# Order of the first transfers and place of one weight's columns in a four-layer graph network kernel

## The chip, the cores and the metric

The kernel runs on one core of a Trainium2 chip. The metric is device time in microseconds (us) of that core, as the median of several executions. One further execution was taken by the hardware profiler; every row and duration below that is called a row of the profile comes from it.

The engines are named as the profile names them: PE is the matrix engine (TensorE), with PEld for its weight loads; DVE is VectorE; ACT is ScalarE; POOL is GpSimd; SP is SyncE, which here only issues transfers (DMAs). Each engine works through its own list of instructions in order and waits at an instruction until its semaphores are there. A DMA is issued by SP, ACT or POOL, each with its own queue; the transfers of all queues run on the same 16 DMA engines.

## The reference, cut to what matters

32 graphs of 512 nodes with 256 features pass through four layers. Each layer normalizes, applies a relu, and adds the result of its graph attention to x. Only layers 0 and 1 bear on the change:

```python
# layer 0: 4 heads of 64
h = jnp.maximum(_layernorm(x, axis=-1), 0.0)
Wh = (X @ W).reshape(B, N, H, F)
e_src = jnp.einsum('bnhf,hf->bnh', Wh, a_src)
e_dst = jnp.einsum('bjhf,hf->bjh', Wh, a_dst)
e = jax.nn.leaky_relu(e_src[:, :, None, :] + e_dst[:, None, :, :], LRELU_ALPHA)
e = jnp.where(mask, e, NEG_INF)
alpha = jax.nn.softmax(e, axis=2)
Hout = jax.nn.elu(jnp.einsum('bijh,bjhf->bihf', alpha, Wh))
# layer 1: one head of 256, softmax over the other axis
h = jnp.einsum('bnf,fo->bno', x, W)
s1 = h @ a1
s2 = h @ a2
e = jax.nn.leaky_relu(s1[:, :, None] + s2[:, None, :], negative_slope=ALPHA)
```

Since `(h W) a = h (W a)`, the scores s1 and s2 can be had as two more columns of the weight: W a1 and W a2. The kernel works these columns out once, at its start, for layer 0 (8 columns) and for layer 1 (2 columns). Layer 2 is another attention over products of h, and layer 3 a transformer block with its own, larger weights.

## The kernel before, in words

All work of the 32 graphs is written out as jobs of a plan (class `Plan`). A job belongs to one engine and has a place, a number; `plan.graph(b)` takes the places of graph b from a table (`PLACES`, with tables of their own for the first three and the last three graphs in `OWN`), and `plan.aside(place)` gives one fixed place to the jobs that follow. `carry_out` sorts all jobs by place and issues them in that order, with a tie from each job to the one before it on the same engine, so that each engine's order within the plan is the table's. What is issued outside the plan (the first loads on ACT's queue, the columns of the weights at L683 to L697) is put among it by the program builder by its own priorities.

Neighbouring graphs overlap: while one graph is in its PE-heavy layer 3, the next ones are in layers 0 to 2.

The start of the program, which the change touches:

- ACT's queue gets six loads in this order: w0 (`w0_t`), w1 (`w1_t`), the rows `src_r` and `dst_r` of layer 0, the rows `a1_r` of layer 1, and the small `a2_t`. A "row" load reads one row of memory once for each of the 128 partitions (`rows_of`, L35). w0 and w1 are 256 KB, `src_r` and `dst_r` 128 KB, `a1_r` 256 KB.
- SP's queue gets graph 0's adjacency (1024 KB), then x of graph 0 (512 KB), then x of graphs 1 and 2, then the transposes of graph 0's mask. The table gives the first two of them place 0, and adjacency comes first since it is the first job of the two.
- POOL's queue gets the weights of layer 3 and other constants (the list `late`, 3.94 MB), each held until x of graph 0 has landed (`plan.load(..., lambda: first)`, where `first` is the job that loads x of graph 0).
- DVE works out the columns: for each half k of the rows of w0, a product with `src_r` or `dst_r` into the scratch tile `wa` (L688) and a sum over each head (L689); for w1, a product with one half of `a1_r` (L694) and a sum (L697). Scratch `wa` is one tile, so a sum always comes between two products.
- DVE also takes the statistics of x for the first norm (`norm_stats`): four `bn_stats` (BATCH_NORM_STATS2 in the profile), four `bn_aggr`, then, after two steps of ACT on `rstd`, three small steps on `newton` and `rstd` and one on `shift`. ACT then writes h of graph 0 in four parts.
- ACT makes the mask `m` from the adjacency as soon as that has landed; SP turns it into `mT` with four transposing DMAs.
- PE transposes h (`ps_t`), multiplies by w0 with its columns (`ps_wh`), and turns the source scores into rows (`ps_sp`, copied by DVE to `spr`, written to memory as `rows_d`, and read back as `rows`, once for each partition). DVE then makes the weights p out of rows, the other scores and mT, and PE multiplies them (`ps_oT`, `ps_den`).
- A few products on PE (`ps_warm`, list `WARM`) are there only to keep PE busy.

Each helper records its operations under one line: L215 for all of ACT's, DVE's and most of POOL's jobs in the plan, L236 for SP's DMAs, L244 for the late weights, L266 for transposes and L268 for products on PE.

Of the kernel before, what the change touches and what calls it, by code (L numbers as in the profile page):

```python
# [11 lines left out]
F32 = mybir.dt.float32  # L12
# [4 lines left out]
OP = mybir.AluOpType  # L17
AX = mybir.AxisListType

P = 128  # L20
# [14 lines left out]
def rows_of(nc, pool, ap, n, name, tag=None, bufs=None, load=None):  # L35

    t = pool.tile([P, n], F32, tag=tag or name, name=name, bufs=bufs)
    (load or nc.scalar.dma_start)(t, bass.AP(tensor=ap.tensor, offset=ap.offset, ap=[[0, P], [1, n]]))
    return t
# [9 lines left out]
def weight_of(nc, pool, ap, name, extra=0, load=None):  # L49

    k, m = ap.shape
    t = pool.tile([P, k // P, m + extra], F32, name=name)
    (load or nc.scalar.dma_start)(t[:, :, :m], ap.rearrange("(k p) m -> p k m", p=P))
    return t
# [229 lines left out]
def width(args):  # L284
# [48 lines left out]

OWN = {
    0: [
        0, 0, 0, 106563, 309, 1073, 1073, 3182, 47382, 297632, 53499, 245689, 52704, 0, 0, 0, 0, 0, 0, 0, 0, 0, 0,
        0, 0, 0, 0, 0, 0, 0, 0, 0, 0, 0, 0, 0, 0, 0, 0, 0, 7, 7, 7, 7, 7, 7, 7, 7395, 1121, 0, 232, 258, 232, 232,
        232, 2502, 1493, 635, 635, 730, 635, 5936, 765, 8516, 3266, 1050, 1050, 1050, 2440, 2440, 17625, 13746,
        2440, 1632, 1889, 1889, 4537, 7572, 7833, 7388, 7395, 7880, 7395, 8585, 9886, 11802, 13679, 12762, 13540,
        13752, 13707, 15308, 14272, 13966, 13966, 16994, 13966, 16169, 16249, 16583, 18584, 18163, 18872, 19087,  # L340
        18927, 18927, 20349, 20349, 20349, 20349, 20352, 20409, 20838, 20907, 20907, 21387, 21387, 21387, 22329,
        23457, 20725, 20923, 23457, 25982, 33376, 34261, 34261, 37292, 34867, 36474, 39879, 41011, 39696, 39709,
        46106, 46400, 46400, 46400, 46675, 46675, 46675, 46675, 49427, 59065, 55989, 56768, 56768, 65040, 68466,
        47867, 47867, 67836, 67836, 69041, 77635, 79329, 79329, 68466, 72704, 72704, 72280, 91934, 91934, 92968,
        92968, 92968, 104578, 95599, 145914, 104578, 105186, 108990, 114563, 157733, 166027, 173427, 174141, 136956,
        151172, 165888, 173979, 136722, 147431, 150754, 153574, 136357, 147891, 158851, 171074, 190479, 191171,
        191171, 196527, 196605, 183067, 183067, 186603, 186603, 187082, 206651, 196694, 196694, 187082, 193870,
        201947, 201947, 187262, 197716, 201947, 206129, 206129, 206129, 207622, 208026, 208026, 208352, 208026,
        219854, 210838, 220497, 220913, 220913, 227229, 217998, 217998, 217998, 226715, 229449, 227967, 229449,
        233286, 233286, 247339, 247339, 247339, 250551, 250856, 251751, 251803, 249399, 228019, 237297, 252726,  # L350
        252726, 252726, 256033, 256033, 256033, 268130, 246835, 246835, 261876, 261876, 261876, 271725, 297107,
        261876, 240354, 240790, 253683, 253683, 253683, 255019, 301246, 309901, 318155, 274295, 278428, 294941,
        305600, 318055, 318055, 299511, 305359, 305359, 320090, 318173, 320554, 305359, 321266, 318173, 321267,
        320641, 321267, 321267, 321267, 321267, 321863, 321863, 326043, 329227, 331562, 332202, 332561, 332561,
        332561, 332922, 330548, 330759, 332506, 332661, 335150, 332802, 406651, 341220, 341466, 342050, 344077,
        344077, 344077, 338280, 338280, 341180, 350371, 353293, 359563, 344829, 344829, 345290, 352882, 355803,
        351180, 351355, 351355, 351355, 360418, 344308, 344308, 344391, 347079, 344345, 350100, 362932, 344061,
        344061, 344061, 344061, 344061, 348875, 362932, 353485, 342050, 343799, 343799, 343799, 343799, 348486,
        365222, 358873, 348973, 348973, 348973, 360911, 348973, 367027, 369940, 367027, 367027, 367638, 367879,
        367879, 385037, 382465, 382465, 394363, 397797, 363107, 363107, 363107, 364066, 363107, 367844, 388551,  # L360
        364560, 364560, 365934, 364560, 370478, 377727, 389387, 379253, 362319, 362411, 362354, 362538, 363348,
        367831, 392522, 386227, 370565, 370565, 370565, 386534, 371732, 387162, 392760, 387162, 393047, 393047,
        396335, 396414, 392760, 398262, 398545, 398803, 406052, 462858, 397797, 406052, 406052, 406052, 407196,
        398293, 406183, 406183, 406183, 407281, 407235, 407281, 407281, 407281, 407235, 407313, 407522, 407522,
        407522, 407522, 407522, 407522, 407522, 407522, 412250, 408973, 413187, 413155, 412853, 413187, 413187,
        413187, 412853, 413349, 413590, 413590, 414897, 416013, 436150, 436742, 421541, 421541, 423055, 415478,
        418099, 421341, 426237, 426237, 427146, 418315, 419286, 419286, 415750, 417007, 417007, 415424, 416349,
        419708, 424205, 424205, 424205, 421266, 421266, 422615, 430070, 430330, 430330, 432660, 432660, 432660,
        432660, 432927, 433724, 433724, 436311, 439075, 439075, 439075, 439075, 439075, 441195, 430355, 430355,
        439081, 440598, 440598, 440653, 440653, 440653, 440653, 440653, 440653, 440653, 440890, 440890, 440972,  # L370
        440977, 443515, 442768, 441195, 443964, 443964, 443964, 441195, 443964, 443964, 443964, 443972, 444016,
        444016, 444016, 444016, 444148, 444142, 444730, 444016, 455955, 462911, 463054, 441529, 533896, 458476,
    ],
    1: [
        -83597, -100000, -83597, 170797, -79776, -79776, -60271, -57701, -52873, 201135, -52847, 76061, 156221,
# [222 lines left out]
def quick_path(  # L598
# [5 lines left out]
    nc = tc.nc  # L604
    B, N, D = x.shape
    NT = N // P
    KD = D // P
# [10 lines left out]
    const = ctx.enter_context(tc.tile_pool(name="const", bufs=1))  # L618
    act = ctx.enter_context(tc.tile_pool(name="act", bufs=1))
# [15 lines left out]
    plan = Plan(tc, PLACES, OWN)  # L635

    def new(tag, name, shape, dtype=F32):
        return plan.tile(K[tag], name, shape, dtype)
# [15 lines left out]
    nc.gpsimd.memset(nshift, -SHIFT)  # L654

    w0_t = weight_of(nc, const, w0, "w0_t", 2 * H0)
    w1_t = weight_of(nc, const, w1, "w1_t", 2)
    src_r = rows_of(nc, act, a0_src, D, "src_r", "half_0")
    dst_r = rows_of(nc, act, a0_dst, D, "dst_r", "half_1")
    a1_r = rows_of(nc, act, a1, 2 * D, "a1_r", "half_2")  # L660
    a2_t = const.tile([P, KD], F32, name="a2_t")
    nc.scalar.dma_start(a2_t, a2[0].rearrange("(k p) o -> p (k o)", p=P))

    late = []

# [19 lines left out]
    for k in range(KD):  # L685
        for a_r, at, sign in ((src_r, D, -1.0), (dst_r, D + H0, 1.0)):
            wa = act.tile([P, N], F32, tag="half_3", name="wa", bufs=1)
            nc.vector.scalar_tensor_tensor(wa[:, :D], w0_t[:, k, :D], sign, a_r, OP.mult, OP.mult)  # L688
            nc.vector.tensor_reduce(  # L689
                w0_t[:, k, at : at + H0], wa[:, :D].rearrange("p (h f) -> p h f", h=H0), AX.X, OP.add  # L690
            )
        for at, sign in ((0, 1.0), (1, -1.0)):
            wa = act.tile([P, N], F32, tag="half_3", name="wa", bufs=1)
            nc.vector.scalar_tensor_tensor(  # L694
                wa[:, :D], w1_t[:, k, :D], sign, a1_r[:, at * D : (at + 1) * D], OP.mult, OP.mult
            )
            nc.vector.tensor_reduce(w1_t[:, k, D + at : D + at + 1], wa[:, :D], AX.X, OP.add)  # L697


    FULL, HALF = 0.858, 0.4315  # L700
# [394 lines left out]
        all_within(seen, graph_mv[0])  # L1095


    plan.aside(max(OWN[0][:2]) + 1)
    for tile_, source in late:
        plan.load(tile_, source, lambda: first)  # L1100
    for place, products in WARM:
# [5 lines left out]
    for b in range(B):  # L1107
        plan.graph(b)
        adj_t = new("adj", f"adj_{b}", [P, NT, N], I32)
        plan.dma(adj_t, adj[b].rearrange("(t p) j -> p t j", p=P), 3.4)  # L1110
        x_t = new("x", f"x_{b}", [P, NT, D])
        job = plan.dma(x_t, x[b].rearrange("(t p) d -> p t d", p=P), 2.0)
        if b == 0:
            first = job
        seen = new("seen", "seen", [P, UPPER])
        graph_mv = [new("mv", "mv", [P, 6, NT, 2]), 0]
        mT, m3 = masks(b, adj_t, seen)
        layer0(b, x_t, mT, seen)
        x_t = layer1(b, x_t, mT, seen)
        layer2(b, x_t, mT, seen)  # L1120
        if b == 0:
            ready = plan.at
        layer3(b, x_t, m3, seen)
# [506 lines left out]
```

## Time and profile before

| What | Value |
|---|---|
| median of 3 runs | 3402.93 us (3396.50 to 3409.46) |
| the profiled execution's own time | 3401.32 us |
| its span, from the first to the last instruction | 3399.4 us |
| PE, DVE, ACT, POOL busy | 3337.5, 2823.3, 2115.3, 11.1 us |
| first instruction of PE | 22.40 us |
| h of graph 0 starts on ACT | 21.69 us |
| graph 0's row copy `spr` | 31.52 us |
| first `ps_oT` of graph 0 | 41.33 us |

Times in rows are counted from the span's start. A row of the timeline gives the start, the length, the engine, the line, the operation, what it writes and reads, how many there are, and in brackets how long its engine stood idle before it and what ended that. "PEclk" in a table of stretches is the granted clock of TensorE, "DMA share" the mean busy share of the 16 DMA engines. In a view of the DMA queues, q1 is SP's, q10 ACT's and q0 POOL's. A row of the chain of waits gives start, length and work of the chain that ended last, followed back from the last instruction to what released it.

The profile as a whole shows PE busy in nine tenths or more of each fortieth of the span but the first and the last:

```profile
## 2 busy tenths in 40 slices
PE   6999999999999999999999999999999999999998
PEld 4565666555665655655655656556556556565555
DVE  6887888888888888888888888888888888887785
```

### The profile page before, as it was taken

To read this page: it belongs to the slowest core of one execution; us is meant where nothing else is said; L and a number is where in the kernel's file an instruction comes from. 1 tells how busy PE (TensorE), PEld (TensorE's weight loads), DVE (VectorE), ACT (ScalarE), POOL (GpSimd) and SP (SyncE) were. 2 spreads that over 40 slices of the span, in tenths; PEclk is the share of its full clock that TensorE was granted. 3 is DMA by queue.
4 is the path that set the end of the run, shared out by engine and by line. 5 is a ranking of instruction groups with operands and counts; after the bars stand their busy time and mean duration, and the time that the engine had idled before them with its cause. 6 is when DMAs were issued, how large, how long until landed. Compare 5 with 4: busy or idle time off the path is not lost.

```text
span 3399.4 us, 48314 instructions
## 1 busy us (share of the span) xinstructions
PE 3337.5 (98%) x17842; PEld 1973.6 (58%) x17842; DVE 2823.3 (83%) x5499; ACT 2115.3 (62%) x4801; POOL 11.1 (0%) x25
## 2 busy tenths in 40 slices
PE   6999999999999999999999999999999999999998
PEld 4565666555665655655655656556556556565555
DVE  6887888888888888888888888888888888887785
ACT  5756666556676556676566665566765667655563
POOL 1000000000000000000000000000000000000000
PEclk9999999999999999999999999999999999999999
DMA  5112110112111111111111112111112111110000
GB/s 165 43 46 57 51 51 28 54 46 57 51 35 40 57 47 57 51 33 42 53 51 51 41 34 57 46 57 51 35 40 65 51 51 42 28 52 26 20 8 27
DMA packets 161171, 161.16 MB, mean 47 GB/s; under 512 B 92576, under 2 KB 126880, under 8 KB 156832
## 3 DMA queue, kind: packets, MB, share of 16 engines
q1 hardware_dynamic: 158464, 153.00, 15.5%
q0 software_dynamic: 1216, 3.94, 0.4%
q8 instruction: 143, 2.34, 0.3%
q10 hardware_dynamic: 1248, 1.05, 0.1%
q14 instruction: 100, 0.82, 0.1%
HBM read 122.96 MB, written 18.22 MB: 42 GB/s over the span
## 4 chain that ended last, share of the span: by engine, by line
PE 81%; DVE 10%; DMA 6%; ACT 3%; issue 1%; SPq 0%; DVEq 0%; ACTq 0%
PE ps_f L268 26%; PE ps_o L268 10%; PE ps_s L268 6%; PE ps_qk L268 6%; PE ps_wh L268 5%; PE ps_ct L268 5%; PE ps_oT L268 5%; DVE p L215 4%; PE ps_t L266 4%; PE ps_e L268 3%; DMA inv<-in_d 3%; PE ps_wo L268 3%; DVE acc L215 3%; PE ps_v L268 2%; PE ps_den L268 2%; PE ps_to L268 1%
## 5 line engine op out<-in xcount | busy, mean ns | idle before, releaser
L215 DVE TENSOR_TENSOR p<-p,m 128x2048 f32<-128x2048 f32 x256 | 578.2, 2278 | 3.8 <-ACT p L215 3.6
L215 ACT ACTIVATE p<-ps_s 128x512 f32<-128x512 f32 x1024 | 554.8, 616 | 40.3 <-PE ps_s L268 36.4
L268 PE MATMUL ps_f<-ff_t,f 128*128 128x256 f32 x2048 | 471.2, 381 | 0.0
L268 PE MATMUL ps_f<-tT,ff_t 128*128 128x512 f32 x1024 | 466.6, 596 | 0.7 <-ACT tT L215 0.7
L268 PEld LDWEIGHTS ps_f<-ff_t,f 128*128 128x128 f32 x2048 | 379.1, 190 | 91.1 <-issue 36.6
L215 ACT ACTIVATE rstd<-mv,eps 128x4 f32<-128x4 f32 x192 | 56.5, 295 | 519.5 <-DVE mv L215 519.5
L215 DVE SCALAR_TENSOR_TENSOR p<-rows,seen,mT 128x512 f32<-128x512 f32 x512 | 352.6, 745 | 31.6 <-PE ps_oT L268 19.3
L215 ACT ACTIVATE h<-x,shift,rstd 128x256 f32<-128x256 f32 x512 | 282.8, 600 | 95.0 <-DVE shift L215 94.7
L268 PEld LDWEIGHTS ps_f<-tT,ff_t 128*128 128x128 f32 x1024 | 185.1, 190 | 194.5 <-issue 154.2
L215 DVE TENSOR_TENSOR acc<-acc,p 128x2048 f32<-128x2048 f32 x128 | 292.8, 2287 | 2.2
L268 PE MATMUL ps_s<-qk 32*128 32x512 f32 x2048 | 287.7, 633 | 1.3 <-ACT qk L215 1.1
L215 ACT ACTIVATE f<-ps_f,ff1b_c 128x512 f32<-128x512 f32 x256 | 168.8, 685 | 132.9 <-PE ps_f L268 125.9
L268 PE MATMUL ps_ct<-p,v 128*32 128x512 f32 x2048 | 245.4, 596 | 0.2 <-ACT v L215 0.2
L268 PE MATMUL ps_o<-h,p 128*128 128x257 f32 x1024 | 245.3, 383 | 0.0
L268 PE MATMUL ps_o<-wh,p 128*128 128x256 f32 x1024 | 242.8, 386 | 0.4 <-ACT wh L215 0.4
L268 PE MATMUL ps_qk<-h3T,wqkv_t 128*128 128x512 f32 x512 | 240.5, 600 | 0.0
L268 PE MATMUL ps_oT<-p,wh 128*32 128x512 f32 x2048 | 239.8, 594 | 0.0
L268 PEld LDWEIGHTS ps_o<-wh,p 128*128 128x128 f32 x1024 | 190.0, 190 | 78.2 <-issue 27.9
L268 PEld LDWEIGHTS ps_o<-h,p 128*128 128x128 f32 x1024 | 189.5, 190 | 51.5 <-PE ps_den L268 19.3
L215 DVE BATCH_NORM_STATS2 st<-x 128x6 f32<-128x256 f32 x512 | 197.3, 413 | 5.6 <-DMA x<-in_x_dram 0.4
L266 PE MATMUL ps_t<-ident,h 128*128 128x128 f32 x1024 | 170.0, 277 | 29.8 <-ACT h L215 29.5
L266 PEld LDWEIGHTS ps_t<-ident,h 128*128 128x128 f32 x1024 | 126.9, 141 | 112.3 <-issue 71.8
(135 smaller groups left out, 4929.9 us busy)
## 6 DMA issues: line engine op xcount, KB each, us to landing
adj<-in_adj_dram SPq DMA_DIRECT2D x32, 1024.0 KB
rows<-rows_d SPq DMA_DIRECT2D x32, 1024.0 KB
x<-in_x_dram SPq DMA_DIRECT2D x32, 512.0 KB
rows<-rows_d SPq DMA_DIRECT2D x32, 512.0 KB
inv<-in_d SPq DMA_DIRECT2D x64, 256.0 KB
out_dram<-y SPq DMA_DIRECT2D x32, 512.0 KB
mT<-m SPq DMA_TRANSPOSE x128
ff_t<-in_L_gnn_W_dram POOLq DMA_DIRECT2D x2, 1024.0 KB, 12.7
```

The lines of the kernel that those rows point to most:

```text
L215: return [getattr(unit, method)(*map(real, args), **{k: real(v) for k, v in kw.items()})]
L266: made.append(self.nc.tensor.transpose(*map(real, c)))
L268: made.append(self.nc.tensor.matmul(*map(real, c[:3]), start=c[3], stop=c[4]))
```

## The change

The first three entries of graph 0's table and its first norm move ahead of the rest: x of graph 0 goes to place -3, adjacency and mask to -2, and fourteen entries (four `bn_stats`, four `bn_aggr`, the two steps of ACT, the four small steps of DVE) from 0 to -2. The loads of `w1_t` and `a1_r` leave ACT's queue for SP's, at place -1. w1's columns become four jobs of the plan at place 8, each one instruction that multiplies and sums (`accum_out`), into a scratch tile of their own, `w1_a`, in place of eight instructions. The job that the late weights wait for is now the adjacency's, not x's. The rest of the large table is only broken into lines anew.

```diff
 OWN = {
     0: [
-        0, 0, 0, 106563, 309, 1073, 1073, 3182, 47382, 297632, 53499, 245689, 52704, 0, 0, 0, 0, 0, 0, 0, 0, 0, 0,
-        0, 0, 0, 0, 0, 0, 0, 0, 0, 0, 0, 0, 0, 0, 0, 0, 0, 7, 7, 7, 7, 7, 7, 7, 7395, 1121, 0, 232, 258, 232, 232,
+        -2, -3, -2, 106563, 309, 1073, 1073, 3182, 47382, 297632, 53499, 245689, 52704, -2, -2, -2, -2, -2, -2,
+        -2, -2, -2, -2, -2, -2, -2, -2, 0, 0, 0, 0, 0, 0, 0, 0, 0, 0, 0, 0, 0, 7, 7, 7, 7, 7, 7, 7, 7395, 1121,
...
     w0_t = weight_of(nc, const, w0, "w0_t", 2 * H0)
-    w1_t = weight_of(nc, const, w1, "w1_t", 2)
     src_r = rows_of(nc, act, a0_src, D, "src_r", "half_0")
     dst_r = rows_of(nc, act, a0_dst, D, "dst_r", "half_1")
-    a1_r = rows_of(nc, act, a1, 2 * D, "a1_r", "half_2")
     a2_t = const.tile([P, KD], F32, name="a2_t")
     nc.scalar.dma_start(a2_t, a2[0].rearrange("(k p) o -> p (k o)", p=P))
+
+    after_adj = []
+    w1_t = weight_of(nc, const, w1, "w1_t", 2, load=lambda *pair: after_adj.append(pair))
+    a1_r = rows_of(nc, act, a1, 2 * D, "a1_r", "half_2", load=lambda *pair: after_adj.append(pair))
+    w1_a = act.tile([P, N], F32, tag="half_4", name="w1_a", bufs=1)
...
                 w0_t[:, k, at : at + H0], wa[:, :D].rearrange("p (h f) -> p h f", h=H0), AX.X, OP.add
             )
-        for at, sign in ((0, 1.0), (1, -1.0)):
-            wa = act.tile([P, N], F32, tag="half_3", name="wa", bufs=1)
-            nc.vector.scalar_tensor_tensor(
-                wa[:, :D], w1_t[:, k, :D], sign, a1_r[:, at * D : (at + 1) * D], OP.mult, OP.mult
-            )
-            nc.vector.tensor_reduce(w1_t[:, k, D + at : D + at + 1], wa[:, :D], AX.X, OP.add)
...
-    plan.aside(max(OWN[0][:2]) + 1)
+    plan.aside(-1)
+    for tile_, source in after_adj:
+        plan.dma(tile_, source, 1.0)
+    plan.aside(8)
+    for k in range(KD):
+        for at, sign in ((0, 1.0), (1, -1.0)):
+            plan.dve(
+                "scalar_tensor_tensor", w1_a[:, :D], w1_t[:, k, :D], sign, a1_r[:, at * D : (at + 1) * D],
+                OP.mult, OP.mult, accum_out=w1_t[:, k, D + at : D + at + 1],
+            )
+    plan.aside(1)
     for tile_, source in late:
         plan.load(tile_, source, lambda: first)
...
-        plan.dma(adj_t, adj[b].rearrange("(t p) j -> p t j", p=P), 3.4)
+        job = plan.dma(adj_t, adj[b].rearrange("(t p) j -> p t j", p=P), 3.4)
         x_t = new("x", f"x_{b}", [P, NT, D])
-        job = plan.dma(x_t, x[b].rearrange("(t p) d -> p t d", p=P), 2.0)
+        plan.dma(x_t, x[b].rearrange("(t p) d -> p t d", p=P), 2.0)
         if b == 0:
             first = job
```

In the built program the lists of the engines differ only at their start. SP's begins with x of graph 0, adjacency of graph 0, `w1_t`, `a1_r`, x of graph 1, x of graph 2, and goes on as before with the transposes. ACT's begins with the loads of `w0_t`, `src_r`, `dst_r` and `a2_t`, then the mask. DVE's begins so (before it, statistics of graphs 0 and 1, L688 to L697 and the cast stood in turns, ahead of graph 0's `newton`):

```
BNStats x0 x4, product w0 src, BNAggr x2, sum, BNAggr x2, product w0 dst, sum,
product w0 src, sum, product w0 dst, cast ident_b, sum,
newton, newton, rstd, shift (graph 0),
BNStats x1 x4, BNAggr x3, product and sum w1 x4,
BNStats x2 x2, BNAggr, newton, newton, rstd, shift (graph 1), copy spr (graph 0), ...
```

POOL's and PE's lists are the same as before.

## The prediction

> **What bounds the kernel now.** I read the engine totals first, then the busy time by stretch, then the chain of waits, and at the end the DMA queues by stretch. By the totals TensorE (PE) is busy 98% of the span of 3399.4 us, so a change at the start can only win what PE loses there. Two stretches hold that:
>
> ```profile
> core 0: us, PE busy (x) PEld busy (x) DVE busy (x) ACT busy (x) POOL busy (x), PEclk, DMA share, GB/s
> 0.00:22.40 22.40, 0.00 (x0) 0.00 (x0) 10.72 (x41) 4.41 (x6) 7.47 (x19) 1.00 0.98 241
> 22.40:41.40 19.00, 16.84 (x67) 12.36 (x71) 5.04 (x20) 12.75 (x47) 3.61 (x6) 1.00 0.80 258
> ```
>
> PE has no instruction at all for 22.4 us while the DMA engines are full. After that it is busy. The chain of waits says what filled the 22.4 us (start, length, what):
>
> ```profile
> 0.75 6.53 DMA adj<-in_adj_dram
> 7.30 7.14 DMA x<-in_x_dram
> 14.46 0.43 DVE st L215
> 14.89 0.32 DVE w_t L697
> ...
> 20.33 0.31 ACT rstd L215
> ...
> 21.69 0.61 ACT h L215
> ...
> 25.15 5.79 PE ps_wh L268 x16
> ...
> 37.57 3.83 PE ps_wh L268 x16
> 41.40 1.85 PE ps_oT L268 x16
> ```
>
> The adjacency comes before x, then VectorE (DVE) works from 12.25 to 20.2 through the statistics of x of graphs 0 and 1 in turns with the weight columns (L688 to L697). Only then does ScalarE (ACT) get rstd, and h of graph 0 starts at 21.69. Three rows of the timeline set the limits of the new order: the mask needs 1.91 us of ACT, the late weights start behind x, and the first p waits for the rows.
>
> ```profile
> 7.31 1.91 ACT L215 ACTIVATE m<-adj 128x2048 bf16<-128x2048 int32 x1 [5.28 <-DMA adj<-in_adj_dram]
> 12.53 0.85 POOL L244 DMA_DIRECT2D wqkv_t<-in_L_gnn_Wqkv_dram  x1 [11.10 <-DMA x<-in_x_dram]
> 38.94 10.69 DVE L215 SCALAR_TENSOR_TENSOR p<-rows,seen,mT 128x512 f32<-128x512 f32 x16 [3.21 <-DMA rows<-rows_d]
> ```
>
> The DMA queues give the paces (packets, MB, share of the 16 engines; q1 is SP's queue, q10 ACT's, q0 GpSimd's). From 6 to 8 us, two streams of 1 KB packets:
>
> ```profile
> q1 hardware_dynamic: 346, 0.38, 57.6%
> q10 hardware_dynamic: 345, 0.34, 51.0%
> ```
>
> That is 358 GB/s, shared packet by packet. From 39 to 43, SP alone with adjacency (2 KB packets), 399 GB/s:
>
> ```profile
> q1 hardware_dynamic: 796, 1.60, 104.0%
> ```
>
> From 8 to 11, beside the rows that are read once for each partition, only 204 GB/s:
>
> ```profile
> q10 hardware_dynamic: 399, 0.36, 68.4%
> q1 hardware_dynamic: 264, 0.26, 28.9%
> ```
>
> From 19 to 22, mask transposes (small packets on q1) beside the late weights (q0), 128 GB/s:
>
> ```profile
> q0 software_dynamic: 95, 0.36, 76.2%
> q1 hardware_dynamic: 90, 0.02, 5.6%
> ```
>
> **The change, part by part.**
>
> *x0 first.* Data start near 2.7 us (0.11 MB by 3.0). x0 (0.52 MB) now shares with w0, src_r and dst_r (0.52 MB) from ACT's queue: 1.05 MB at 358 GB/s is 2.9 us, so its data end at 5.6. From last byte to first use I take 1.0 us (adjacency: 0.96 MB by 6.0, so all by about 6.3, used at 7.31). x0 is usable at 6.6 instead of about 12.2. If the slow stretch of 8 to 11 comes again beside it, it costs 3 x (1 - 204/358) = 1.3 us: 7.9.
>
> *Mask second.* 1.05 MB at 399 GB/s is 2.6 us: usable at 5.6 + 2.6 + 1.0 = 9.2 (slow 10.5), two to three us later than now. In ACT's order m still stands ahead of rstd: 9.2 + 1.91 = 11.1, and the two rstd steps need 0.57 (20.33 to 20.90): 11.7 (slow 13.0).
>
> *DVE.* Ahead of graph 0's newton steps there remain, in the built order, four statistics (1.41 at 57.83), the eight w0 instructions of L688 and L689 in dependent pairs at 0.46 (9.64 to 10.10), four aggregates (0.36) and the identity cast (0.14 in its row's spacing). Gone from there are graph 1's four statistics, three aggregates and w1's eight instructions. 6.6 + 1.41 + 3.68 + 0.36 + 0.14 = 12.2 (slow 13.5). So DVE ends last, 0.5 us behind ACT: shortening either alone would give nothing more than that. From newton to h is 21.69 - 20.90 = 0.79: h of graph 0 at 13.0 (slow 14.3), a gain of 8.7 to 7.4. I take 8.0, the middle, since the same row broadcasts run again but may fall beside the mask.
>
> *w1's columns behind the norm.* Eight instructions become four with accum_out, 0.42 + 0.08 (accumulator read at 77.84) each: 2.0 us. With x1's statistics and aggregates (1.8) and half of x2's (0.9) DVE works 4.7 us from 13.0 to 17.7. It is hidden by ACT and PE: graph 1's newton came 30.14 - 21.69 = 8.4 us behind h, so it is due at 21.4. 3.7 us are spare; beyond that, queued behind are newton of graph 1 and spr (L215), and with spr the rows of graph 0.
>
> *Queues.* ACT loses two DMA issues (about 0.5 each) while it would idle anyway. SP gains two between mask and x1; x1's issue now waits for x0 (6.6) instead of the mask (7.3), so nothing is lost. w1, a1_r and x1 are 1.05 MB more, 2.9 us: x1 is usable at 5.6 + 2.6 + 2.9 + 1.0 = 12.1, x2 1.5 later, slow ends 14.7 and 16.2. DVE wants x1 at 13.0 to 14.3, x2 near 17. Nothing, or 0.4 out of the 3.7 spare.
>
> *GpSimd's late weights* now wait for the mask (9.2) instead of x (12.2). Their first bytes come 3.4 us behind the issue (12.53, none before 16), so at about 12.7, as x2 ends. First use is far off (128.14, ps_bv).
>
> *mT and rows.* The transposes start behind m at 11.1 to 12.4 (now 9.24), behind x2 in SP's queue, and share all their time with the late weights. Alone, 567 packets went within 33 to 35 us, so three times 512 need some 5 us: 19. p needs them at 38.94 - 8.0 = 30.9. The fourth transpose and the rows follow spr at 23.8 and now meet the tail of the weights: between 28 and 33 that tail moved 0.60 MB, 120 GB/s, which would stretch the rows' 2.5 us (414 GB/s from 36 to 38) by 0.7. Cover: p is ready at 39.69 and PE wants it at 41.40, 1.7 us. I take 0; the upper end is the rival below.
>
> The Trainium skill ("DMA: Bandwidth & Descriptors", section on queues, rings and completion order) speaks against this change: an engine turns between queues packet by packet, so each small transpose packet would wait for a large weight packet. The row of 19 to 22 (95 against 90) agrees, those of 16 to 18 (112 against 279) don't. By the rule the transposes could end no sooner than the weights, whose 3.94 MB at 406 GB/s (23 to 25) end at 22.4: an estimate that still leaves the 30.9 untouched and the sum as it is.
>
> *Downstream.* From spr on all five engines run the same instructions in the same order, so the start shifts the rest one for one. PE's slow first products (5.79 against 3.83 for 16) shift along.
>
> The same skill ("TensorE: Matmul & The Clock Gate", Part 1) calls the activity window free-running, 3.4 us long; by it the slow start could vary by some 1.7 us either way, an estimate. No row here shows the phase.
>
> **Sum.** The profiled execution took 3401.32 (1.9 outside the span); minus 8.0 it is 3393.3. The median, 3402.93, lies 1.6 higher, and I forecast 3395 on its level.
>
> **Rivals.**
> 1. *Transposes starve beside the weights (slower than before).* If the pace of 19 to 22 (30 transpose packets and 0.128 MB per us) held for all weights, these would last 31 us, to 43.5. By then 920 of 1,536 packets are through; the rest (290 per us) takes 2.1, the fourth 1.8, the rows 3.5: 50.9 instead of 32.6 (30.9 + 1.7). 18.3 late, less 8.0: 3413. It turns to a loss once the rows land 9.7 us late. For it: the pace is in the trace. Against: at 14 to 15 and 18 to 19 q1 passed 403 and 402 packets in one us, and the weights at 406 GB/s from 23 to 25. Chance 0.06.
> 2. *The mask holds ACT.* If the mask gets only 204 GB/s throughout, it is usable at 5.6 + 5.1 + 1.0 = 11.7, rstd done at 14.2, h at 15.0, gain 6.7; with x0 late as well 5.4: 3397.5. For it: m before rstd in ACT's order. Against: 399 GB/s once alone. 0.10.
> 3. *Hidden anyway.* The gain is given back before graph 1's products at 37.57, because x1 or x2 comes over 4 us late: gain under 2, 3401.5. For it: x1 and x2 now stand behind 0.52 MB more in SP's queue (w1 and a1_r), and the late weights start sooner. Against: 3.7 us of cover. 0.06.
>
> **How the numbers follow.** Forecast 0.78, at 3392 to 3399 by its own bounds. The three runs lie 6.5 to either side of their median, so I widen by that much of scatter. Low 3384, high 3407: rival 1 and tails of the scatter stay out. 0.5% is 17 us, about what a measurement of this kernel can tell from no change; the whole gain is half of it. Faster by over 0.5% needs under 3385.9: about 1 in 6 of the forecast by scatter, 0.13. Slower needs over 3419.9: part of rival 1 and scatter, 0.04. Within: 0.83.
>
> **What would show it.** First BATCH_NORM_STATS near 6.6 to 7.9; m at 9.2 to 10.5; h of graph 0 at 13.0 to 14.3; first PE 0.75 behind it; spr near 23.8; p near 30.9 with PE not waiting; ps_oT near 33.4; the span shorter by what h came earlier. I am wrong if x0 lands with the mask, if DVE idles before spr waiting for x1 or x2, if p waits for mT or rows beyond 32.6, or if the shift at ps_oT is not found again at the end.

## The result, and the profile after

| | before | after |
|---|---|---|
| median of 22 executions each | 3401.62 us (3396.50 to 3411.23) | 3395.68 us (3391.62 to 3404.88) |
| ratio, 95% interval | | 0.9983 (0.9976 to 0.9989) |
| profiled execution, its span | 3401.32, 3399.4 us | 3394.89, 3392.9 us |
| h of graph 0 | 21.69 us | 14.48 us |
| spr of graph 0 | 31.52 us | 23.89 us |
| first p | 38.94 us | 34.35 us |
| first ps_oT | 41.33 us | 35.25 us |

The changed kernel is 5.8 us faster by the ratio (0.17% of 3400; by the interval 3.7 to 8.2). The start won more than that: 7.2 us at h, 7.6 at spr, but only 4.6 at p. The view of stretches, cut at PE's first product and at the first ps_oT, as for the kernel before:

```profile
core 0: us, PE busy (x) PEld busy (x) DVE busy (x) ACT busy (x) POOL busy (x), PEclk, DMA share, GB/s
0.00:15.20 15.20, 0.00 (x0) 0.01 (x1) 6.00 (x24) 4.31 (x6) 4.60 (x15) 1.00 0.85 259
15.20:35.25 20.05, 16.44 (x64) 12.03 (x65) 7.14 (x35) 13.96 (x52) 6.51 (x11) 1.00 1.06 297
```

The stretch without PE fell from 22.40 to 15.20 us. The second one grew from 19.00 to 20.05, with 0.4 us less of PE's work in it: PE idles more there than before. The chain of waits says on what (start, length, what):

```profile
14.48 0.61 ACT h L215
...
17.93 5.39 PE ps_wh L268 x16
...
23.89 0.28 DVE spr L215
...
24.20 4.61 DMA rows_d<-spr
...
28.83 5.38 DMA rows<-rows_d
...
34.35 0.76 DVE p L215
...
35.25 2.52 PE ps_oT L268 x14
```

In the kernel before, the chain ran over ACT and PE from h to ps_oT. Now it runs over two transfers: `rows_d`, 8 KB, takes 4.6 us to land, and `rows` land 5.4 us after that. The timeline shows two waits that delay the start, a longer one at the norm (DVE waited 0.89 us for `dst_r` in the kernel before) and a new one at PE:

```profile
7.70 0.43 DVE L692 SCALAR_TENSOR_TENSOR wa<-w_t,src_r 128x256 f32<-128x256 f32 x1 [0.42 <-DMA src_r<-in_L_gnn_a_src_dram]
11.07 0.42 DVE L692 SCALAR_TENSOR_TENSOR wa<-w_t,dst_r 128x256 f32<-128x256 f32 x1 [2.33 <-DMA dst_r<-in_L_gnn_a_dst_dram]
11.17 1.91 ACT L215 ACTIVATE m<-adj 128x2048 bf16<-128x2048 int32 x1 [9.14 <-DMA adj<-in_adj_dram]
13.70 0.15 DVE L215 SCALAR_TENSOR_TENSOR newton<-mv,rstd 128x4 f32<-128x4 f32 x1
34.35 2.08 DVE L215 SCALAR_TENSOR_TENSOR p<-rows,seen,mT 128x512 f32<-128x512 f32 x3 [6.24 <-DMA rows<-rows_d]
35.25 1.19 PE L268 MATMUL ps_oT<-p,wh 128*32 128x512 f32 x6 [1.46 <-DVE p L215]
```

DVE waits 2.33 us for the row `dst_r` and then ACT's mask starts at 11.17, so h is late. Later PE stands 1.46 us for p. It loses some more behind that, as its products then follow DVE's 16 p one by one: 11.84 us from the first p to the first copy of oT, of which DVE's p alone take 10.69. At that copy (46.19 against 51.05) the shift is 4.9 us, and at graph 2's spr (64.19 against 69.03) still 4.8.

The span of the profiled execution is 6.5 us shorter, but that does not follow from the 4.8 in one step. A piece of half clock that the kernel before has at 134 to 140 us (granted clock 0.50 from 136 to 138), and the changed one hasn't, lifts the shift to 6.5 at the spr at 175 us. Then it falls to 3.3 at 731 and 0.8 at 1558, and is 6.7 again at 2977. In between PE waits now and then for DVE's `cT`, a tile of layer 3, and not in the same graphs in both: 7.7 us in the changed kernel against 4.4 from 170 to 1560, but 1.0 against 5.3 from 1900 to 2700. That is the larger part of the drift. So the span of one execution does not say what the start is worth; the medians do, within their interval.

### The profile page after: what moved, and what is told of

The parts are those of the page before. It is cut to its first block, busy times and chain, and to the rows that moved or that the text cites. A ratio compares the mean times of both kernels' runs of the same rounds, so it can differ in the third digit from the quotient of the medians.

```text
span 3392.9 us, 48312 instructions
## 1 busy us (share of the span) xinstructions
PE 3336.8 (98%) x17842; PEld 1970.8 (58%) x17842; DVE 2821.7 (83%) x5499; ACT 2117.1 (62%) x4801; POOL 11.1 (0%) x25
## 3 DMA queue, kind: packets, MB, share of 16 engines
q8 instruction: 142, 2.33, 0.3%
## 4 chain that ended last, share of the span: by engine, by line
PE 83%; DVE 8%; DMA 5%; ACT 3%; issue 1%; SPq 0%; DVEq 0%; ACTq 0%
PE ps_f L268 26%; PE ps_o L268 11%; PE ps_s L268 7%; PE ps_qk L268 6%; PE ps_ct L268 5%; PE ps_oT L268 5%; PE ps_wh L268 5%; PE ps_t L266 4%; DVE p L215 4%; PE ps_e L268 3%; PE ps_wo L268 3%; PE ps_den L268 3%; PE ps_v L268 3%; DVE acc L215 2%; DMA inv<-in_d 2%; PE ps_to L268 1%
```

## The experiments

Theory A at the outset: the gain at spr is real, and it is given back between spr and p since the mask's transposes and the rows share the 16 DMA engines with the late weights. The rivals: the columns on DVE, the mask, or something downstream. All marks below come from one profiled execution each, "gain" from the ratio of medians times 3400 us, with its 95% interval; "shift" is how much earlier than before the mark comes. "Held" means that all fifteen late loads wait for graph 0's rows.

| Kernel | h | spr | p | spr to p | shift at the first oT copy | ratio (95%) | gain |
|---|---|---|---|---|---|---|---|
| before | 21.69 | 31.52 | 38.94 | 7.42 | | | |
| after | 14.48 | 23.89 | 34.35 | 10.46 | 4.9 | 0.9983 (0.9976 to 0.9989) | 5.8 (3.7 to 8.2) |
| all late loads held | 13.72 | 22.27 | 29.38 | 7.11 | 9.0 | 0.9973 (0.9963 to 0.9983) | 9.2 (5.8 to 12.6) |
| columns only | 19.08 | 28.50 | 39.03 | 10.53 | 0.2 | 1.0001 (0.9992 to 1.0009) | -0.3 (-3.1 to 2.7) |
| order only | 16.07 | 24.49 | 33.97 | 9.48 | 5.2 | 0.9984 (0.9975 to 0.9993) | 5.4 (2.4 to 8.5) |
| norm first | 9.07 | 19.71 | 34.44 | 14.73 | 3.7 | 0.9994 (0.9985 to 1.0003) | 2.0 (-1.0 to 5.1) |
| norm first, held | 8.97 | 19.69 | 26.89 | 7.20 | 11.6 | 0.9976 (0.9966 to 0.9985) | 8.2 (5.1 to 11.6) |
| columns only, held | 19.13 | 27.56 | 34.65 | 7.09 | 3.7 | 0.9996 (0.9987 to 1.0005) | 1.4 (-1.7 to 4.4) |
| before, held | 21.70 | 30.59 | 38.14 | 7.55 | 0.7 | 1.0003 (0.9994 to 1.0012) | -1.0 (-4.1 to 2.0) |
| held, a_t late | 14.04 | 23.49 | 30.88 | 7.39 | 8.0 | 0.9980 (0.9971 to 0.9989) | 6.8 (3.7 to 9.9) |
| norm first, held, a_t late | 8.85 | 19.85 | 27.02 | 7.17 | 9.0 | 0.9963 (0.9949 to 0.9976) | 12.6 (8.2 to 17.3) |
| small loads held | 13.76 | 22.80 | 29.70 | 6.90 | 8.5 | 0.9971 (0.9960 to 0.9983) | 9.9 (5.8 to 13.6) |

**All late loads held.** The fifteen late loads wait for graph 0's rows instead of its adjacency.

```diff
-    for tile_, source in late:
-        plan.load(tile_, source, lambda: first)
...
+    held = rows_jobs[0]
+    plan.aside(held.place[0] + 1)
+    for tile_, source in late:
+        plan.load(tile_, source, lambda: held)
```

> The changed kernel with one edit: the late weights on POOL's queue wait for graph 0's rows (the transfer that DVE's first p waits for) instead of graph 0's adjacency. Theory A: in the changed kernel the mask transposes take turns with the late weights, drain only when those end, and hold rows_d, the fourth transpose and the rows behind them in SP's queue, so that p starts at 34.35, 10.46 us behind spr, where it was 7.42 before the change. Without the weights beside them the distance is 7.4 again: spr stays at 23.9, rows are issued 2.6 us behind rows_d, p starts at 31.0 to 31.8, graph 1's first ps_den (62.88 now) comes near 60, and the time is 2 to 3 us below the changed kernel's (near 3393), if the weights do no new harm to the adjacency of graphs 1 and 2, which they now meet. Rival B: the way through memory is slow by itself when it starts this early (writing rows_d and reading it back), whatever runs beside it: p stays near 34 and the time near 3395.7.

p follows spr after 7.11 us instead of 10.46 and PE doesn't wait for it: p comes 5.0 us sooner than in the changed kernel, and the shift at the oT copy is 9.0. So the late set takes the 3 us. Which of its loads, this run can't say. Of the 4.1 us between the two shifts 1.6 were there at spr already: h came 0.8 sooner, as `dst_r` was used at 10.31 instead of 11.07, which is before the first packet of the late set (13.35 in the changed kernel); and PE's first 16 products took 4.67 us against 5.55. From spr on the holding is worth 2.5 us. The times alone do not show it, as the intervals of the two gains overlap.

**Columns only, order only.** The first leaves the order of the transfers as before and only moves w1's columns behind the norm (the four `accum_out` instructions at place 8); the second keeps the new order but works w1's columns out at the old place, with loads from ACT's queue.

```diff
 # columns only, against before
-        for at, sign in ((0, 1.0), (1, -1.0)):
...
-            nc.vector.tensor_reduce(w1_t[:, k, D + at : D + at + 1], wa[:, :D], AX.X, OP.add)
+    plan.aside(8)
...
+                OP.mult, OP.mult, accum_out=w1_t[:, k, D + at : D + at + 1],
 # order only, against after
-    w1_t = weight_of(nc, const, w1, "w1_t", 2, load=lambda *pair: after_adj.append(pair))
+    w1_t = weight_of(nc, const, w1, "w1_t", 2)
...
```

> The kernel before with one part of the change: w1's columns become the four jobs behind graph 0's norm. The loads keep their queues and order (adjacency first), the norm its place. Theory A: DVE's work between x's landing and newton loses eight instructions at 0.33 to 0.46, so h of graph 0 starts near 18.6 instead of 21.69, a gain of 3.1; the weights start where they did (12.5), the rows come 7.4 to 8 us behind spr, and p gains some 2.5 to 3: time near 3399. Rival C: the columns were hidden behind the landing of x of graph 1 and the whole gain is the order of the transfers: h gains under 1 us, time as before, near 3401.6.

> The changed kernel without the part on w1: its weight and rows are loaded on ACT's queue and its eight column instructions stand ahead on DVE, as before the change; x of graph 0 first, its mask second, norm ahead, late weights behind the adjacency as changed. Theory A: DVE now waits for src_r, dst_r and then a1_r in ACT's queue before newton; a1_r lands near 13, so newton near 15 and h near 16.5 (14.48 in the changed kernel, 21.69 before); spr near 26; the rows are late as in the changed kernel, p near 35.5 to 36.5, time near 3397.5. Rival C (the order is the whole gain): h near 14.5 and time near 3395.7. If the columns were the whole gain: h over 20, time near 3401.

The columns alone bring 2.6 us at h and 3.0 at spr, and nothing at p, where 2.5 to 3 were expected. The order alone has the whole gain of the change, though its h comes 1.6 us later than in the changed kernel: p is at 33.97 and 34.35 all the same, where 35.5 or later was expected. From spr on, then, p did not follow DVE's work in either.

In the run with the columns alone the delay sits at another place of SP's queue:

```profile
28.80 0.36 SPq L236 DMA_DIRECT2D rows_d<-spr  x1
...
30.53 0.50 SPq L236 DMA_DIRECT2D rows<-rows_d  x1
```

`rows_d` is through after 1.73 us, as the three transposes were done (q1 passes nothing from 24 to 29). But the fourth transpose (512 packets) stands ahead of `rows`, and from 29 to 33 us the whole queue passes only 573 packets.

**Norm first.** Graph 0's norm goes ahead of w0's columns on DVE, and ACT's mask goes behind h (place 0.5).

```diff
-    -2, -3, -2, 106563, 309, ...
+    -2, -3, 0.5, 106563, 309, ...
...
+            plan.dve("scalar_tensor_tensor", wa[:, :D], w0_t[:, k, :D], sign, a_r, OP.mult, OP.mult)
```

> The changed kernel with two edits: ACT's mask step stands behind h of graph 0 and the first half of its transpose instead of ahead of rstd, and w0's columns are worked out on DVE behind shift instead of between the statistics and newton. Theory A: h of graph 0 starts near 8.9 (5.88 + 1.41 + 0.36 + 0.57 + 0.79), the first ps_wh only when the columns are there, near 14 (17.75 in the changed kernel), spr near 20, 3.9 us sooner. But the transposes still drain only when the weights end, so p starts at 33.5 to 34.5 and the time stays within 1 us of the changed kernel's, 3394.5 to 3396. Rival B (the distance of 10.46 from spr to p is a property of the way through memory): p at 30.5, time near 3392. Rival D (only spr sets p, with 7.4): p at 27.5, time near 3389.

This is the strongest sign against any cause on DVE or ACT: spr comes 4.2 us sooner than in the changed kernel and p not at all (34.44). The mask, at 12.20 now instead of 11.17, is not the reason: it is at 12.10 when the late loads are held as well, and p comes at 26.89. The edit costs something in addition. PE idles longer before p, and its timeline and stretches show what follows:

```profile
35.34 4.20 PE L268 MATMUL ps_oT<-p,wh 128*32 128x512 f32 x16 [5.47 <-DVE p L215]
```

```profile
34.00:36.00 2.00, 0.67 (x4) 0.31 (x8) 1.56 (x3) 0.00 (x0) 0.00 (x0) 0.50 0.99 382
36.00:38.00 2.00, 2.00 (x14) 0.89 (x14) 2.00 (x4) 0.68 (x1) 0.00 (x0) 0.50 1.02 391
```

After 5.47 us without work the granted clock is 0.50 from 34 to 38 us, and 16 products of ps_oT take 4.20 us instead of the 1.92 of the run with all loads held. The shift at the copy is 3.7, less than in the changed kernel.

**Norm first and held; columns only and held; before and held.** The same edits, combined.

> The changed kernel with two edits: graph 0's norm goes to VectorE ahead of w_t's columns, and the five late weights wait for graph 0's rows. Theory A (the transposes and the rows share the DMA engines with the late weights): the norm first brings h0 near 9.1 and spr near 19.7, as in the run with the norm alone, and with no weights beside the transposes rows and p follow spr by about 7.1 us as in the run with the weights held, so p near 27 instead of 34.4, and a median 2 to 3 us below the run with the weights held (3392.15), near 3389 to 3390. Rival D (something else than the weights, the mask's own chain, sets p once the norm is early): m at 12.2 as in the run with the norm alone, p not before 30, and a time near 3392. Rival E (TensorE goes cold while it waits for p): p near 27 but a second half-clock stretch, and no gain over 3392.

> The kernel before with two edits: layer 1's weight columns leave the head for graph 0's first norm (as in the run with the columns alone), and the late weights wait for graph 0's rows. Theory A: spr near 28.5 as with the columns alone, p 7.1 us behind it, near 35.6 instead of 39.0, and the time 3 us or so below that of before, near 3397. Rival F (the columns are worth nothing even without the weights beside the transposes): p stays near 39 and the time stays that of before.

> The kernel before with one edit: the late weights wait for graph 0's rows. Theory A: in the kernel before the distance from spr to p is 7.4 us, close to the 7.1 without the weights, so spr alone sets p, holding the weights changes nothing: spr near 31.5, p near 38.6, time within 0.5 us or so of before. Rival G (the weights cost the start of the kernel before as well, or holding them brings something further on, such as less traffic beside graph 1's adjacency): a gain of 2 us or more.

In all three p follows spr after 7.1 to 7.6 us, as theory A had it: with the late loads away, every microsecond at spr arrives at p. In the kernel before, holding the loads gives 0.7 at the oT copy and nothing that the time shows: there spr came late enough. The columns are worth another 3.0 at the copy then (3.7 in all), against 0.2 with the late loads in the way; that is by the marks, as the interval of their time (-1.7 to 4.4) holds nothing as well. The times expected of the first two were a little too good: 8.2 us gained where some 10 were expected, 1.4 where 3 were. The intervals still hold the shifts at the copy (11.6 just at the upper end), so whether a part is lost further on stays open. Norm first is the one pair in which the times too speak for the holding, though their intervals touch: 2.0 (at most 5.1) without it, 8.2 (at least 5.1) with it.

**Small loads held.** The late set is four big weights (3 MB) and, behind them, eleven small loads (the text below counts ten): five columns of 1 to 4 KB in 4-byte packets, and six rows of 1 KB that are each read 128 times. Here only the small ones wait for graph 0's rows.

```diff
-    for tile_, source in late:
+    for tile_, source in late[:4]:
         plan.load(tile_, source, lambda: first)
...
+    for tile_, source in late[4:]:
+        plan.load(tile_, source, lambda: held)
```

> The changed kernel with the late set split: the four big weights (3 MB, packets of 4 and 6 KB) start as in the changed kernel, the ten small loads behind them (columns in 4-byte packets, rows) wait for graph 0's rows. Theory A (the transposes take turns with the big weights' packets; the small loads only slow the rest): most of the give-back stays, distance from spr to p between 8.6 and 10.5 us against 7.1 without any weights, p between 32.5 and 34.4, and the time within 2 us of the changed kernel's. Rival L (the small loads are what holds the transposes back): the distance falls to 8 us or less, p at 31.5 or sooner, and the time moves 2 to 3 us towards the run with all of them held.

Theory A falls in the form in which it named the weights; the rival is right, with 6.90 us from spr to p. The big weights stay beside the transposes and cost p nothing. The time, a gain of 9.9 (5.8 to 13.6), fits this, but its interval overlaps that of the change: it is the marks that show it. The DMA queues show both halves of it (packets, MB, share of 16 engines; q0 is the late set, q1 SP's). From 18 to 20 us, in this run and then in the changed kernel:

```profile
q0 software_dynamic: 202, 0.78, 95.2%
q1 hardware_dynamic: 202, 0.05, 11.4%
```

```profile
q0 software_dynamic: 166, 0.64, 83.1%
q1 hardware_dynamic: 169, 0.04, 10.5%
```

Beside the big weights the transposes go one for one with them, in both kernels: about 100 and 85 packets a us. From 22 to 24, in the same order of kernels:

```profile
q1 hardware_dynamic: 1012, 0.24, 105.4%
q0 software_dynamic: 62, 0.20, 26.0%
```

```profile
q0 software_dynamic: 221, 0.55, 94.8%
q1 hardware_dynamic: 242, 0.05, 13.9%
```

Here the weights are through and the transposes run at 506 packets a us; in the changed kernel q0 goes on and they stay at 121. By the counts the 1,536 packets of the first three transposes are through near 26.6 us there and near 24 in this run, an estimate, as the queue's packets are not told apart. `rows_d`, which stands behind these three in SP's queue, lands only after them: 4.61 us in the chain above, where 1.80 us pass between the issues of `rows_d` and `rows` in this run (SP's timeline):

```profile
23.11 0.36 SPq L236 DMA_DIRECT2D rows_d<-spr  x1
...
24.91 0.43 SPq L236 DMA_DIRECT2D rows<-rows_d  x1
```

The view of the issues gives, for the changed kernel, what the small loads took from issue to landing (last number, us), beside a weight:

```profile
wqkv_t<-in_L_gnn_Wqkv_dram POOLq DMA_DIRECT2D x1, 768.0 KB, 6.8
...
bo_r<-in_L_gnn_bo_dram POOLq DMA_DIRECT2D x1, 128.0 KB, 9.6
...
bqk_c<-in_L_gnn_bqkv_dram POOLq DMA_DIRECT2D x1, 2.0 KB, 10.6
```

2 KB behind the weights take longer than 768 KB at their head. The run with the columns alone shows the same without any big weight beside: there the late queue had moved 3.23 MB by 28 us, more than the big weights' 3.15, and it was beside the small loads alone that the fourth transpose crept. Whether the 4-byte columns or the rows read 128 times weigh more was not tried apart.

**The slow stretch at 8 to 11 us: rows exchanged, a_t late, distinct rows.** In every kernel the DMA's rate falls there, and it made `dst_r` and the mask late. Three edits on top of the run with all loads held: `src_r` and `dst_r` change places in ACT's queue; `a_t` (256 packets of 4 bytes, behind `dst_r`) joins the late set; and, with that, both rows are read from 128 different rows of w0 (layer 0's columns are then other numbers, the work is the same).

```diff
+    late.append((a2_t, a2[0].rearrange("(k p) o -> p (k o)", p=P)))
...
-    dst_r = rows_of(nc, act, a0_dst, D, "dst_r", "half_1")
+    dst_r = act.tile([P, D], F32, tag="half_1", name="dst_r", bufs=None)
+    nc.scalar.dma_start(dst_r, w0[P:, :])
...
```

> The run with the weights held, with src_r's and dst_r's loads exchanged on ScalarE's queue. The second of these two loads was slow (a 1 KB packet took 117 to 194 ns against 46 to 48 ns for the first), at 8 to 10 us. If it is the place in the queue or the moment: src_r, now second, lands last and VectorE waits for it as it waited for dst_r, about 11 us. If it belongs to dst_r's data or its tile: dst_r's packets stay slow, now at 5 to 8 us, and src_r's are 46 to 48 ns. VectorE's first use is of src_r, so the time may move by some tenths; no gain is expected.

> The run with the late weights held behind graph 0's rows, with one more edit: a_t, 1 KB that is read in 256 packets of 4 bytes on ScalarE's queue right behind dst_r, is loaded with the late weights. In every run so far the DMA's rate falls from some 380 GB/s to 60 to 240 GB/s at about 8 to 11 us, just while these packets are under way, whichever of src_r and dst_r goes second. Theory H (the 4-byte packets cause the slow stretch): without them the rate stays near 350 GB/s until x of graph 2 is asked for, the adjacency lands at 9.2 to 9.7 us instead of 10.5, so m near 9.5, VectorE waits less than 0.5 us for dst_r instead of 1.55, h0 near 12.5 instead of 13.7, p 1 to 1.5 us sooner than 29.4, and the time up to 1 us lower than 3392.15. Rival I (the broadcast rows or the start of the adjacency cause it): the rate still falls at 8 us, m stays at 10.5, h0 at 13.7.

> The run with norm first and weights held, with a_t loaded with the late weights as well. Theory H: m near 9.5 instead of 12.1 (or when ScalarE is through with h at 11.0, if h goes first), mT and seen sooner, spr no later than 19.7; p stays 7.1 us behind spr, near 26.9, as spr's own path over h does not wait for the adjacency. By the spans so far 12 us won at p are worth 8 in the time, so 3392 to 3393, no more than the run without this edit, and no less. If theory H falls, all marks are those of that run.

> The run with a_t late, with src_r and dst_r read from w0's 128 upper and 128 lower rows instead of one row of a0_src and a0_dst read 128 times; the attention columns of layer 0 are therefore other numbers, the work is the same. The slow stretch at 8 to 11 us stayed when the 4-byte packets were gone, and hit whichever of the two rows came second. Theory J (128 reads of one row of memory cause it): without them the rate stays above 300 GB/s, dst_r is usable before 8.7 and m near 9.5. Rival K (something else at that moment, the same in every kernel): the rate still falls to some 100 GB/s near 8 us, VectorE still waits 1.5 to 2.8 us for dst_r, m near 10.8.

With the rows exchanged, DVE waits 2.75 us for `src_r`: it is the second row that is late, whichever it is. Without a_t's packets the mean rate from 8 to 11 rises from 182 to 262 GB/s, but DVE still waits 2.15 us for `dst_r` and m stands at 10.76: theory H falls for the waits. With the norm first and the loads held the same edit takes the rate only from 175 to 210, and `dst_r` is used 1.4 us later (11.43 against 10.04). With distinct rows the rate is 340 GB/s, and most of the wait is gone (the timeline of that run):

```profile
9.29 0.42 DVE L694 SCALAR_TENSOR_TENSOR wa<-w_t,dst_r 128x256 f32<-128x256 f32 x1 [0.59 <-DMA dst_r<-in_L_gnn_W_dram]
9.42 1.91 ACT L215 ACTIVATE m<-adj 128x2048 bf16<-128x2048 int32 x1 [7.38 <-DMA adj<-in_adj_dram]
```

m at 9.42 is what theory J said, and h comes at 12.70. `dst_r` is used at 9.29, where theory J wanted 8.7. So the 128 reads of one row of memory go with the slow stretch, by one execution of that run. It also reads another tensor, w0, and that these rows lie elsewhere in memory is a rival that was not tried. Why only the second such load suffers stays open; the first of them ran at some 46 ns a packet in the changed kernel.

Norm first, held, with a_t late has the best time of all, 3382.98 us against 3396.12 for the kernel before on that chip, from five executions; its interval (0.9949 to 0.9976) touches that of the change itself (0.9976 to 0.9989). Its start does not say why it should beat the same kernel with a_t at its old place: the marks up to p are within 0.2 us, and PE even ran at half clock (0.61 and 0.54 in the two stretches from 20 to 28 us), which put its first ps_oT 2.5 us later. What its profile has less of is PE's waits for `cT` from 110 to 3000 us: 4.2 us against 9.8 with a_t at its old place and 10.5 in the kernel before. Nothing ties these to a_t. No gain was expected of a_t here, and the two intervals don't tell one from none.

## Why the prediction was right, and where it was not

It forecast 3395 and got 3395.68, but two terms of its sum were off, both to the same side: 8.0 us of gain were taken, and 4.9 arrived at the first oT copy. The level hid a part of it, as the kernel before has 3401.62 over 22 executions and not the 3402.93 that the forecast stood on; the gain is 5.8. That the number came within 1 us is in part luck, then; that the change gains some us by the order of the transfers is not. One of its own signs of being wrong came true: p waited for the rows until 34.35, beyond 32.6.

- *x0 first*: right in kind, and better than its range: the first statistics stand at 5.88, before the 6.6 to 7.9 forecast.
- *Mask second*: 11.17, beyond the slow end of 10.5. The slow stretch did come again, beside the mask and `dst_r`, at 187 GB/s, and its price was counted for 1.3 us; it was about 2 us against the fast end. The distinct rows (with a_t away too) gave 9.42, near the 9.2 worked out without it, so the arithmetic held and the chosen middle did not.
- *DVE ends last, by 0.5*: they ended within 0.3 us of each other (ACT's rstd at 13.51, DVE's last sum at 13.78), since `dst_r` and the mask were late together. h came at 14.48, 0.2 beyond the slow end: gain 7.2 where 8.0 was taken.
- *w1's columns behind the norm*: right that they are hidden there (DVE waits 0.50 us for x1, and spr isn't late). But of the change's gain they made nothing that shows: the order alone had the same p within 0.4 us and the same time within the intervals. They are worth something only when p follows spr.
- *mT and rows, "I take 0"*: the step that failed, by its size. The cover was put at 1.7 us, and the delay was 3.0 at p and 2.8 on PE's path (1.46 of wait and the rest in step with DVE's p). The cover holds for the first product only: DVE needs 10.69 us for its 16 p and PE 9.72 from the first ps_oT to the copy, so from p to the copy it was 12.11 us before and 11.84 after, a cover of 0.3. The prediction saw that the fourth transpose and the rows "meet the tail of the weights" and priced that tail at 0.7 us on the rows' own transfer. It missed that `rows_d` stands in SP's queue behind transposes not yet through, and that the tail is eleven loads which move little and hold the transposes up for long. The run with only these held shows 6.90 us from spr to p in place of 10.46.
- *The rule on turns between queues* (Trainium skill, "DMA: Bandwidth & Descriptors", section on queues, rings and completion order): the row from 18 to 20 us, 169 against 166 packets, agrees with it. The estimate made of it, that this "still leaves the 30.9 untouched", was right for the big weights: with them alone p came at 29.70. It left out what stands behind them in the same queue.
- *GpSimd's late weights*: issued from 11.45 on, not 9.2, as they wait for the slow adjacency; their first packets came 1.9 us behind that and not 3.4.
- *Downstream one for one*: wrong from spr to p, where 3.0 us were lost. From the first oT copy on it fits and is not shown: in all eleven comparisons of the table the interval of the gain holds the shift there (once just at its end), but the intervals are 4.5 to 9 us wide and hold the shift at p in ten of them. In single profiles the shift wanders by several us, for the larger part through PE's waits for `cT`.
- *PE's slow first products*: they did not just shift along. In the timeline the 16 took 5.96 us in the kernel before, 5.55 in the changed one and 4.56 to 5.58 in the other profiles where they ran in one piece, with the granted clock at 1.00 in all these rows, so up to 1.4 us at spr come from there.
- *Rivals*: the first, transposes starved beside the weights, is the right place with a price six times too high; the second, the mask holding ACT, came true in part (m at 11.17 of the 11.7 it named, h 0.8 us later than taken); the third, x1 or x2 over 4 us late, did not (0.50 us of wait for x1). None of them decided the sign.

## What to carry to other kernels

When a start is pulled forward, follow each transfer behind the new mark to its place in its own queue, and ask what is still ahead of it there; 3.0 us won at spr were worth 0.2 at the oT copy with the queue in the way, and 4.0 were worth 3.7 without. Price a load by the time in which it keeps others waiting and not by its bytes: here the rows read once for each partition and the 4-byte columns, 0.8 MB together, cost p some 3.5 us, and the 3 MB of weights nothing. Measure a shift behind the last wait of the start, here at the first copy of oT, and leave what comes later to the medians.

## What was not expected of the hardware

- Two rows of memory, each read 128 times, went with a slow stretch for every queue: from 8 to 11 us 262 GB/s (210 in another kernel) with a_t away, 340 with distinct rows of another tensor in their place; and the second such load was late (2.15 us of wait against 0.59) while the first was not.
- 256 packets of 4 bytes went with a lower rate over these three us in both pairs that differ by them (182 against 262 GB/s, 175 against 210), though each packet's own record is some 9 ns long and no wait became shorter without them.
- A view's releaser can be wrong: the chain after gives h at 14.48 to the transfer of x (5.87, 8.58 us long), but DVE's shift ended at 14.44 by its own row, and x had been in use since 5.88.
- Half a clock came and went between kernels that run the same products (at 134 to 140 us in the kernel before, nowhere there in the changed one, between 84 and 100 in five of the runs with all loads held). The granted clock of the three 2-us slices from 134 to 140 (0.78, 0.50, 0.86) makes it some 3.4 us of half clock, 1.7 us lost, so spans of single profiles don't tell effects of that size apart.
